# Queries of seven pairs of batches by seven block products for eight (fp32), on one core

## The chip, the cores and the metric

The kernel runs on one core of one Trainium2 chip. The metric is the device time of one execution in microseconds (us), the median of a few runs. The engines are named as in the profile: PE (TensorE, matrix products), DVE (VectorE), ACT (ScalarE), POOL (GpSimd) and SP (SyncE, which issues most transfers). Everything is fp32.

## What is computed

A cross attention for 16 batches of 100 rows of width 640, with 8 heads of 80, against a context of 718 rows of width 384 and 4 more tokens. Cut to what matters:

```
query = hidden_states @ Wq                       # 16 x 100 x 640, Wq 640 x 640
keyt, valt = enc @ Wk, enc @ Wv                  # enc 16 x 718 x 384
hs = mha(query, keyt, valt)
ca_q1 = einsum('btc,th->bch', ca, Wq_ca)[:, indices]
ca_hs1 = mha(ca_q1, residual, residual)          # residual = hidden_states
ca_hs2 = mha(ca_hs1 @ Wq, ca @ Wk_ca, ca @ Wv_ca)
out = (hs + ca_hs2) @ Wout + b_out + residual
```

The change concerns the first line, for batches 2 to 15.

## The kernel before

The program is one list of instructions per engine, in the order in which the code calls them: before the loop a scheduler places them, and from `tc.manual_schedule` (L1235) on each engine keeps the program's order. The loop over the batches b = 0 to 15 is a software pipeline. In stage b PE runs, in this order: the scores of batch b (L609, three groups, queries times keys), then the value products of batch b and the key products of batch b + 1 mixed (L434, L465), the last column chunk of the keys (`last_keys`, L559), in some stages the output projection of two tiles of 128 rows (`project_pair`, L1033 to L1088), in odd stages the queries of the next pair of batches (`queries`, L531 to L551), and the products of the exponentials with the values (a_ps, L1456). The odd stages are b = 1, 3, 5, 7, 9, 11, 13; an output pair is projected in b = 3, 6, 8, 11, 13.

Keys, values and the projection of output pairs already run by schemes with fewer block products: sums of blocks are made ahead (of the context by POOL in `enc_sums`, L481 to L500, thirteen additions per batch; of the weights once), the products go to several PSUM banks, and DVE or ACT add each bank to the results that need it (L403 to L408, `read` in L1059). In `project_pair` DVE makes nine such reads from four banks, and PE goes on in a bank only when its reads are done.

The queries are plain before: `queries` makes one of five chunks of 128 output columns, as five matmuls of 128x128 weights with the rows of both batches (200 columns), and ACT copies the chunk from PSUM to `qp` or, for the fifth, twice with a mask to `qz` (L543, L547). The fifth output chunk holds the last 16 columns of each head.

DVE and POOL in the second half of an odd stage: DVE adds value and key banks, makes the third subtraction of the maximum (`subtract(2)`, L1258, 120 x 1600), then the maximum of the other attention's scores `e1` in steps (`Maximum`, L684 to L730: transpose, reduction, small reductions, spread, transpose) and subtracts it (L815); `softmax1(n)` makes the next n steps. The spread is made by ACT where the other attention's batch follows an output pair, else by DVE (L720 to L727). POOL multiplies and adds values of the small attention (`values2`, L892, L899), issues two loads, makes `keys` (L745, five small products) and then `enc_sums` for the context of batch b + 2. Its next work is `scores1` of the next stage (L798). `enc` is a tile of 15 places of 240 columns: seven for the raw context, which transfers fill, and eight that `enc_sums` fills.

The end of the second half of an odd stage is called in this order (L1390 to L1440): `subtract(2)`, `exponential(2)`, `last_keys`, [`softmax1(3)`, `project_pair`], `softmax1`, `keys`, `enc_sums`, `queries`, `exponentials1`, then a_ps.

Of the kernel before, what the change touches and what calls it, by code (L numbers as in the profile page):

```python
# [10 lines left out]
ALU = mybir.AluOpType  # L11
# [7 lines left out]
P = 128  # L19
# [107 lines left out]
def kernel(  # L127
# [33 lines left out]
    def pair(name):  # L161
        tile = ps2.tile([P, 2, 512], F32, tag="ps2", name=name)
        return tile
# [224 lines left out]
    class Blocks:  # L388


        def __init__(self, plan):
            self.opened, self.begun = {}, set()
            self.plan = iter(enumerate(plan))
            self.ends = {bank: k for k, (bank, _, _) in enumerate(plan)}
# [156 lines left out]
                )  # L551


    def chunk_keys(n, banks, weights, enc):
# [197 lines left out]
    class Second:  # L752
# [56 lines left out]
        def softmax1(self, n=8):  # L809

            if not self.top:
                self.top = Maximum(e1, f"1_{self.b}", self.b - 2 in PAIRS)
            self.top.go(n)
            if self.top.over is not None:
                nc.vector.tensor_tensor(e1[:S], e1[:S], self.top.over[:S], ALU.subtract)  # L815
# [97 lines left out]
    class Last:  # L913
# [109 lines left out]
        def sums(self):  # L1023

            r = PAIRS[self.b]
            one, two = hsTs[r], hsTs[r + 1]
            for out, left, right, op in (
                (sum1, two[:, :2], two[:, 2:4], ALU.add),
                (two[:, :2], sum1, one[:, :2], ALU.subtract),
            ):  # L1030
                nc.gpsimd.tensor_tensor(out, left, right, op)

        def project_pair(self):  # L1033

# [12 lines left out]
            def product(to, terms, first):  # L1047
                steps = [(t[:, c], f[:, c]) for t, f in terms for c in range(t.shape[1])]
                for i, (t, f) in enumerate(steps):
                    nc.tensor.matmul(  # L1050
                        to[:, : H // 2],
                        t,
                        f,
                        start=first and i == 0,
                        stop=i == len(steps) - 1,
                        skip_group_check=True,
                    )

            def read(bank, j, k):  # L1059
                part = xn[r + j][:, k * (H // 2) : (k + 1) * (H // 2)]  # L1060
                nc.vector.tensor_tensor(part, bank[:, : H // 2], part, ALU.add)

            product(b1, [(one[:, :2], w(0, 0))], True)
            read(b1, 0, 0)
            product(b2, [(one[:, 2:4], w(1, 0)), (one[:, 4:], last(0))], True)
            read(b2, 0, 0)
            nc.gpsimd.tensor_tensor(one[:, 2:4], one[:, 2:4], two[:, :2], less)
            product(b1, [(two[:, :2], wout2[:, 0])], False)
            read(b1, 1, 0)
            nc.gpsimd.tensor_tensor(two[:, :2], two[:, 2:4], two[:, :2], less)  # L1070
            nc.gpsimd.tensor_tensor(wout2[:, 0], wout2[:, 0], w(0, 0), less)
# [164 lines left out]
    for b in range(B):  # L1236
# [28 lines left out]
        def exponential(i):  # L1265
            nc.scalar.activation(st[i], st[i], AF.Exp, scale=SCALE)  # L1266
# [60 lines left out]
        elif b + 1 < B:  # L1327
# [61 lines left out]
                m_next = load_m(b + 2)  # L1389
            subtract(2)  # L1390
            exponential(2)
            last_keys(b + 1, enc)
            if b + 2 < B:
                enc_next = load_rest(b + 2, enc_next)
# [1 line left out]
                last.transpose()  # L1396
            if last.b in PAIRS:
                second.softmax1(3)
                last.project_pair()
                if last.b == max(PAIRS):  # L1400
                    nc.sync.dma_start(
                        out=forms[1],
                        in_=wout[: 2 * P, H // 2 :].rearrange("(c p) n -> p c n", p=P),
                    )
            second.softmax1()
        else:
            room = enc_tile("spare").rearrange("p f k -> p (f k)")
            spare.extend(room[:, i * H : (i + 1) * H] for i in range(2))
# [22 lines left out]
            last.project()  # L1431
        if 0 < b < B - 2:
            keys(m_next)
            enc_sums(enc_next)
        if b % 2 and b + 1 < B:
            xT, tiles = xT_at[0], queries_tiles(p + 1)
            for n in range(HC):
                queries(p + 1, xT, tiles, n)
        if 0 < b < B - 1:
            second.exponentials1()  # L1440

# [37 lines left out]
        if b + 2 < B:  # L1479
            second_next.products()  # L1480
            second_next.copy()
        if 0 < b < B - 2:
            mine.turn()
        last = mine
# [55 lines left out]
```

## Time and profile before

| | |
|---|---|
| Median of three runs (lowest, highest) | 925.86 us (924.5 to 927.1) |
| The profiled execution | 925.05 us |
| Its span, first to last instruction | 923.3 us |
| PE busy | 916.2 us, 99% |
| DVE busy | 679.9 us, 74% |
| POOL busy | 682.1 us, 74% |
| ACT busy | 434.2 us, 47% |
| Query products (L535) on PE | 400 records, 69.1 us |

In rows of the profile, `out<-in` are the program's tiles with their numbers left out (enc<-enc is a sum made in the context's tile), then the shapes, the count, and after the bar the busy time, the mean duration of one in ns, and the idle time of the engine before them with what ended it. Rows of the timeline begin with the start and the duration in us, and instructions of one kind that follow each other are merged into one row (x50). PE's fp32 matmuls stand as two records each; PEld is the loading of weights, which runs beside the products. Records of PE overlap, so that the duration of one is longer than its share of PE's time.

### The profile page before, as it was taken

The numbers are of one execution on the slowest core, as the hardware profiler recorded it, in microseconds if no ns is written. First come the engines' busy times: TensorE is split into PE (matmuls) and PEld (weight loads), VectorE is DVE, ScalarE is ACT, GpSimd is POOL, SyncE is SP. The second block draws the span as 40 slices with busy tenths as digits, with TensorE's granted clock in tenths as the row PEclk, the third lists the DMA queues.
The fourth block names the chain that finished last, engine by engine and source line by source line (L and its number), as shares of the span: only waits on it lengthen the run. The fifth ranks groups of instructions, "written<-read, shape, count | busy, mean of one in ns | idle before, by whom it ended". The sixth has DMA issues, their size and how long they took to land.

```text
span 923.3 us, 26190 instructions
## 1 busy us (share of the span) xinstructions
PE 916.2 (99%) x11290; PEld 772.4 (84%) x11290; DVE 679.9 (74%) x1085; ACT 434.2 (47%) x836; POOL 682.1 (74%) x647
## 2 busy tenths in 40 slices
PE   9999999999999999999999999999999999999998
PEld 6988889788797979888798787988879888797866
DVE  2459795888739896795967859579883898838883
ACT  2234543737327373552636536264641737427341
POOL 5749999788947878497784968757996588956723
PEclk9999999999999999999999999999999999999999
DMA  8822013050300404032030310205031050310201
GB/s 258 262 94 78 25 43 100 2 156 2 103 31 13 116 3 131 3 92 65 19 115 4 103 54 30 76 2 154 3 90 43 2 155 2 104 45 2 82 20 41
DMA packets 49675, 62.85 MB, mean 68 GB/s; under 512 B 14072, under 2 KB 38200, under 8 KB 49560
## 3 DMA queue, kind: packets, MB, share of 16 engines
q1 hardware_dynamic: 45512, 51.49, 18.4%
q0 software_dynamic: 3024, 8.53, 3.0%
q8 instruction: 89, 1.46, 0.7%
q10 hardware_dynamic: 1024, 1.15, 0.4%
q14 instruction: 26, 0.21, 0.1%
HBM read 55.59 MB, written 5.57 MB: 66 GB/s over the span
## 4 chain that ended last, share of the span: by engine, by line
PE 96%; DVE 3%; DMA 1%; issue 0%; POOL 0%; ACTq 0%; DVEq 0%; POOLq 0%
PE a_ps L1456 12%; PE s_ps L609 12%; PE v_psA L434 10%; PE v_psB L434 8%; PE kT_ps L559 8%; PE k_psA L465 8%; PE q_ps L535 7%; PE k_psB L465 6%; PE o_ps L1050 5%; PE v_psC L434 3%; PE k_psC L465 3%; PE v_ps L375 2%; PE v_psD L434 2%; PE v_psE L434 2%; PE y_ps L773 1%; PE k_psD L465 1%
## 5 line engine op out<-in xcount | busy, mean ns | idle before, releaser
L798 POOL TENSOR_TENSOR e<-ca,g 100x800 f32<-100x800 f32 x64 | 97.9, 1540 | 125.1 <-ACT kT L407 82.1
L500 POOL TENSOR_TENSOR enc<-enc 128x240 f32<-128x240 f32 x135 | 109.5, 820 | 18.2 <-DMA enc<-in_enct 11.1
L1258 DVE TENSOR_TENSOR st<-st,over 120x1600 f32<-120x1600 f32 x48 | 119.1, 2482 | 0.0
L1456 PEld LDWEIGHTS a_ps<-vs,st 120*36 120x36 f32 (+3 forms) x3072 | 109.2, 125 | 4.9 <-issue 4.8
L1456 PE MATMUL a_ps<-vs,st 120*36 120x81 f32 (+3 forms) x3072 | 112.0, 233 | 0.0
L434 PE MATMUL v_psA<-wv_sb,enc 128*120 128x320 f32 x352 | 109.3, 433 | 0.0
L899 POOL TENSOR_TENSOR hs<-hs,hs 100x640 f32<-100x640 f32 x48 | 100.6, 2095 | 3.8
L805 POOL TENSOR_TENSOR e<-e,e 100x800 f32<-100x800 f32 x48 | 93.6, 1950 | 3.8
L892 POOL TENSOR_TENSOR hs<-vb,p 100x640 f32<-100x640 f32 x64 | 88.0, 1386 | 5.9 <-DMA vb<-va_d 3.0
L434 PE MATMUL v_psB<-wv_sb,enc 128*120 128x320 f32 x296 | 91.9, 433 | 0.0
L1266 ACT ACTIVATE st<-st 120x1600 f32<-120x1600 f32 x48 | 73.9, 1539 | 37.0 <-DVE st L1258 36.9
L465 PE MATMUL k_psA<-enc,wk_sb 128*128 128x240 f32 x360 | 89.2, 371 | 0.0
L434 PEld LDWEIGHTS v_psA<-wv_sb,enc 128*120 128x120 f32 x352 | 64.2, 183 | 25.0 <-issue 0.5
L465 PEld LDWEIGHTS k_psA<-enc,wk_sb 128*128 128x128 f32 x360 | 67.2, 190 | 15.0
L1270 DVE TENSOR_TENSOR most<-most,st 120x800 f32<-120x800 f32 x64 | 67.6, 1056 | 15.9 <-ACT st L659 14.8
L609 PE MATMUL s_ps<-qp,kT 64*56 64x100 f32 (+1 forms) x3072 | 73.5, 248 | 0.0
L465 PE MATMUL k_psB<-enc,wk_sb 128*128 128x240 f32 x300 | 73.0, 366 | 0.0
L434 PEld LDWEIGHTS v_psB<-wv_sb,enc 128*120 128x120 f32 x296 | 54.1, 183 | 21.9 <-DVE vs L405 0.4
L609 PEld LDWEIGHTS s_ps<-qp,kT 64*56 64x56 f32 (+1 forms) x3072 | 67.1, 130 | 5.5 <-issue 4.2
L965 ACT COPY hsT<-turned_hs 32x160 f32<-32x160 f32 (+7 forms) x244 | 67.7, 278 | 3.0
L535 PE MATMUL q_ps<-xT,wq_sb 128*128 128x200 f32 x400 | 69.1, 333 | 0.0
L535 PEld LDWEIGHTS q_ps<-xT,wq_sb 128*128 128x128 f32 x400 | 67.8, 190 | 1.0 <-issue 0.5
(168 smaller groups left out, 1766.1 us busy)
## 6 DMA issues: line engine op xcount, KB each, us to landing
vb<-va_d POOLq DMA_DIRECT2D x32, 250.0 KB, 3.8
vb<-va_d SPq DMA_DIRECT2D x32, 250.0 KB
enc<-in_enct SPq DMA_DIRECT2D x30, 240.0 KB
enc<-in_enct SPq DMA_DIRECT2D x15, 360.0 KB
xT<-in_xt SPq DMA_DIRECT2D x8, 500.0 KB
rest<-in_enct SPq DMA_DIRECT2D x31, 120.0 KB
xn<-in_x SPq DMA_DIRECT2D x11, 320.0 KB
out<-xn SPq DMA_DIRECT2D x11, 320.0 KB
```

What stands on the lines that cost most here:

```text
L434: nc.tensor.matmul(at[0][j][:KN, : H // 2], a_form(self.enc, f)[:, j * KN : (j + 1) * KN], wv_there.get(f, wv_sb[:, W_AT[f]]), start=first ...
L465: nc.tensor.matmul(at[:, i * KT : (i + 1) * KT], wk_sb[:, W_AT[f], i], a_form(self.enc, f), start=(first and i == 0), stop=last, skip_grou ...
L500: nc.gpsimd.tensor_tensor(out, left, right, op)
L535: nc.tensor.matmul(q_ps[:, : 2 * S].rearrange("p (j s) -> p j s", j=2), wq_sb[:, c, n * P : (n + 1) * P], xT[:, :, c, :], start=(c == 0), ...
L609: nc.tensor.matmul(s_ps[at][k0:k1, cols], w, rhs, start=not begun & {(at, k) for k in range(k0, k1, 32)}, stop=last, skip_group_check=True,)
L798: first = nc.gpsimd.tensor_tensor(to, self.ca[:, t, :].unsqueeze(1).to_broadcast([S, NH, S]), g[:, :, t].unsqueeze(2).to_broadcast([S, NH, ...
L805: nc.gpsimd.tensor_tensor(e, e, to, ALU.add)
L892: first = nc.gpsimd.tensor_tensor(to, self.vb[t][:S].rearrange("p (h d) -> p h d", h=NH), p2[:, :, t].unsqueeze(2).to_broadcast([S, NH, D] ...
L899: nc.gpsimd.tensor_tensor(sums, sums, to, ALU.add)
L1258: return nc.vector.tensor_tensor(st[i], st[i], top.over[:KN].unsqueeze(1).to_broadcast([KN, 2, ROWS]), ALU.subtract,)
L1266: nc.scalar.activation(st[i], st[i], AF.Exp, scale=SCALE)
L1456: nc.tensor.matmul(a_v[lo:hi, h % 4], st[i // 2][: KEYS[i], i % 2, h * S + lo : h * S + hi], block(i, h // 4)[: KEYS[i], h % 4], start=(i ...
```

## The change

The queries of batches 2 to 15, two at a time, are made by a scheme of seven products. The four output chunks and the four input chunks of 128 are halved into blocks of 256, and the two batches are the third dimension of two: seven products of a block of weights (`wq_block(g, c)`) with a block of rows take the place of eight. The fifth input chunk (`rest`) is added plainly for each output block and batch, and the fifth output chunk is made plainly for both batches. All matmuls have 64 weight columns, in two halves of the array (k = 0 and 64).

Three sums of weights and four of rows are needed. One of the weights is made once, in place, at the end of b = 0. The other sums are made by DVE for each pair (`sums`: w2, w3, then t1 to t4), in the eight places of the next context's tile that `enc_sums` fills later; so `enc_sums` is now called behind the query products. w2 is renewed once between the products. Without an output pair (b = 1, 5, 7, 9) the six sums stand right behind `subtract(2)` and `exponential(2)`; with one (b = 3, 11, 13) they stand behind the first three reads in `project_pair`: w2 behind the first, w3 behind the second, t1 to t4 behind the third. Of the softmax of the other attention, one step (`between(1)`) stands on DVE behind the renewed w2 and ahead of two additions of results, and the rest behind. Four banks are read by ACT copies, and five additions by DVE bring the other reads. The banks are two pairs and both `psk` banks, where the five chunks before took `psk` and `ps1` banks in turn.

```diff
+    def wq_block(g, c):
+        return wq_sb[:, 2 * c : 2 * c + 2, 2 * g * P : 2 * (g + 1) * P]
+
+    class Queries:
+        def __init__(self, p, xT, enc):
+            self.p, self.xT = p, xT
+            room = enc[:, len(A_RAW) :].rearrange("p f k -> p (f k)")
+            part = lambda lo, n: room[:, lo : lo + 2 * n].rearrange(
+                "p (c n) -> p c n", c=2
+            )
+            self.w2, self.t1 = part(0, 2 * P), part(4 * P, S)
+            lo = 3 * KT
+            self.w3 = part(lo, 2 * P)
+            self.t3, self.t2, self.t4 = (
+                part(lo + 4 * P + 2 * i * S, S) for i in range(3)
+            )
+
+        def v(self, c, m):
+            return self.xT[:, m, 2 * c : 2 * c + 2]
+
+        def sums(self, steps=range(3)):
+            v, less = self.v, ALU.subtract
+            for step in steps:
+                for out, left, right in (
+                    [(self.w2, wq_block(1, 0), wq_block(0, 0))],
+                    [(self.w3, wq_block(1, 1), self.w2)],
+                    [
+                        (self.t1, v(0, 1), v(0, 0)),
+                        (self.t2, v(1, 1), self.t1),
+                        (self.t3, v(1, 1), v(0, 1)),
+                        (self.t4, v(1, 0), self.t2),
+                    ],
+                )[step]:
+                    nc.vector.tensor_tensor(out, left, right, less)
+
+        def product(self, bank, weights, moving, first):
+            steps = [(c, i) for c in range(weights.shape[1]) for i in range(2)]
+            for n, (c, i) in enumerate(steps):
+                for k in (0, 64):
+                    nc.tensor.matmul(
+                        bank[k : k + 64, i * S : (i + 1) * S],
+                        weights[:, c, i * P + k : i * P + k + 64],
+                        moving[:, c],
...
+        def rest(self, bank, g, m, first):
+            weights = wq_sb[:, 4:, 2 * g * P : 2 * (g + 1) * P]
+            self.product(bank, weights, self.xT[:, m, 4:], first)
+
+        def make(self, tiles, between):
...
+            one = pair(f"q_ps1_{p}")
+            two = pair(f"q_ps2_{p}")
+            a, b = psumk(f"q_psA_{p}"), psumk(f"q_psB_{p}")
+            f, c, e, d = one[:, 0], one[:, 1], two[:, 0], two[:, 1]
...
+            def add(bank, g, m):
+                nc.vector.tensor_tensor(q(g, m), full(bank), q(g, m), ALU.add)
+
+            for ch in range(HC):
+                for k in (0, 64):
+                    nc.tensor.matmul(
+                        full(f)[k : k + 64],
+                        wq_sb[:, ch, 4 * P + k : 4 * P + k + 64],
+                        self.xT[:, :, ch, :],
...
+            for u in range(2):
+                nc.scalar.mul(
+                    qz[:, 0, :, u * S : (u + 1) * S], full(f), qmask[:, u : u + 1]
+                )
+            self.product(a, w(0, 0), v(0, 0), True)
+            nc.scalar.copy(q(0, 0), full(a))
+            self.rest(c, 0, 0, True)
+            self.product(c, w(0, 1), v(1, 0), False)
+            add(c, 0, 0)
+            self.product(a, self.w2, self.t2, False)
+            nc.vector.tensor_tensor(self.w2, w(0, 1), self.w2, ALU.subtract)
+            between(1)
+            self.rest(e, 1, 0, True)
+            self.product(e, w(1, 1), self.t4, False)
+            nc.scalar.copy(q(1, 0), full(e))
+            add(a, 1, 0)
+            self.product(b, self.w3, self.t3, True)
+            add(b, 1, 0)
+            self.rest(d, 0, 1, True)
+            self.product(d, self.w2, v(1, 1), False)
+            nc.scalar.copy(q(0, 1), full(d))
+            self.rest(b, 1, 1, False)
+            nc.scalar.copy(q(1, 1), full(b))
+            between(8)
+            self.product(a, w(1, 0), self.t1, False)
+            add(a, 0, 1)
+            add(a, 1, 1)
...
@@ class Second, softmax1
+            if self.top.over is not None:
+                return
             self.top.go(n)
...
@@ class Last, project_pair
-        def project_pair(self):
+        def project_pair(self, others):
+            others = iter(others)
...
                 nc.vector.tensor_tensor(part, bank[:, : H // 2], part, ALU.add)
+                for other in others:
+                    other()
+                    break
...
@@ the loop
             subtract(2)
             exponential(2)
+            if b % 2:
+                mixed = Queries(p + 1, xT_at[0], enc_next[0])
+                if last.b not in PAIRS:
+                    mixed.sums()
             last_keys(b + 1, enc)
...
-                last.project_pair()
+                last.project_pair(
+                    [lambda n=n: mixed.sums([n]) for n in range(3)] if b % 2 else []
+                )
...
-            second.softmax1()
+            if b % 2:
+                second.softmax1(1 if last.b in PAIRS else 3)
+            else:
+                second.softmax1()
...
         if 0 < b < B - 2:
             keys(m_next)
-            enc_sums(enc_next)
         if b % 2 and b + 1 < B:
             xT, tiles = xT_at[0], queries_tiles(p + 1)
-            for n in range(HC):
-                queries(p + 1, xT, tiles, n)
+            mixed.make(tiles, second.softmax1)
+        if 0 < b < B - 2:
+            enc_sums(enc_next)
...
+        if b == 0:
+            nc.vector.tensor_tensor(
+                wq_block(1, 0), wq_block(1, 0), wq_block(1, 1), ALU.add
+            )
```

More of the change, by code (lines that the diff above doesn't have):

```diff
@@ L551, in queries, with q, full @@
                 )
+    def wq_block(g, c):
[37 more added lines that the diff above has]
+                        moving[:, c],
+                        start=first and n == 0,
+                        stop=n == len(steps) - 1,
+                        skip_group_check=True,
+                    )
[3 more added lines that the diff above has]
+        def make(self, tiles, between):
+            qp, qz = tiles
+            p, v, w = self.p, self.v, wq_block
+            one = pair(f"q_ps1_{p}")
+            two = pair(f"q_ps2_{p}")
+            a, b = psumk(f"q_psA_{p}"), psumk(f"q_psB_{p}")
+            f, c, e, d = one[:, 0], one[:, 1], two[:, 0], two[:, 1]
+            def q(g, m):
+                return qp[:, g, :, m * S : (m + 1) * S]
+            def full(bank):
+                return bank[:, : 2 * S].rearrange("p (i s) -> p i s", i=2)
+            def add(bank, g, m):
[6 more added lines that the diff above has]
+                        self.xT[:, :, ch, :],
+                        start=(ch == 0),
+                        stop=(ch == HC - 1),
+                        skip_group_check=True,
+                    )
[26 more added lines that the diff above has]
+            add(a, 1, 1)
@@ L1398 @@
                 second.softmax1(3)
-                last.project_pair()
+                last.project_pair(
+                    [lambda n=n: mixed.sums([n]) for n in range(3)] if b % 2 else []
+                )
                 if last.b == max(PAIRS):
@@ L1481 @@
             second_next.copy()
+        if b == 0:
+            nc.vector.tensor_tensor(
+                wq_block(1, 0), wq_block(1, 0), wq_block(1, 1), ALU.add
+            )
         if 0 < b < B - 2:
```

## The prediction

> **What bounds the kernel now.** I read the page first (span, busy shares, granted clock, chain), then the chain in order of time, then the timeline of single stages. The profiled execution took 925.05 us, of which the span is 923.3; it lies 0.8 us under the median of 925.86. All sums are made against 925.05. About 0.3%, 2.8 us, is what a measurement of this kernel can tell from no change.
>
> ```profile
> span 923.3 us, 26190 instructions
> PE 916.2 (99%) x11290; PEld 772.4 (84%) x11290; DVE 679.9 (74%) x1085; ACT 434.2 (47%) x836; POOL 682.1 (74%) x647
> PEclk9999999999999999999999999999999999999999
> PE 96%; DVE 3%; DMA 1%; issue 0%; POOL 0%; ACTq 0%; DVEq 0%; POOLq 0%
> ```
>
> TensorE is busy for 99% of the span at full granted clock, and the chain that ended last is 96% PE. So two things alone move the end: less PE work, and a wait put in front of PE. DVE and POOL each have a quarter free, but only where nothing is due.
>
> **PE work.** The query projection and its neighbours:
>
> ```profile
> 357.60 8.46 PE q_ps L535 x50
> 366.06 6.92 PE a_ps L1456 x191
> L609 PE MATMUL s_ps<-qp,kT 64*64 64x100 f32 x1536 | 73.4, 248 | 0.0
> ```
>
> Each fp32 matmul stands as two records. A pair of batches takes 25 full matmuls of 200 columns: 50 records in 8.46 us, 0.338 per matmul. The change needs, in halves of 64 weight columns that run beside each other: 5 of 200 columns for the fifth output chunk, 8 of 100 for the fifth input chunk (`rest`), and 7 products of 4 each for the rest, 36 of 100 in all. No row shows 128x64 weights with 100 columns. The nearest: a_ps runs such halves with 81 columns, 96 record pairs in 6.92 us, 0.072 each; q_ps has 0.169 per record at 200. A line through both gives 0.0875 at 100 columns, 0.175 per matmul. By the column rate of q_ps it would be 0.169; by s_ps, whose 3072 records run four at a time, 73.4/768 = 0.096, so 0.191. I take 0.175, as a_ps has the same tiles. That makes 5 x 0.338 + 36 x 0.175 = 7.99 us against 8.46: **-0.47 us per pair, -3.3 for seven** (ends: -4.8 and +0.8). A product of four is 0.70, a `rest` 0.35. From the start Q of the query stage the order is: fifth output chunk until Q+1.69, product a 2.39, rest and product c 3.44, second product on a (needs w2, t2) 4.14, rest and product e (t4) 5.19, product b (w3, t3) 5.89, rest d 6.24, product d (needs the renewed w2) 6.94, rest b (needs DVE's read of b) 7.29, last product 7.99.
>
> **Who must keep up.** DVE now makes six sums ahead (two of 512 elements, four of 200), renews w2 and adds five results. This is b = 5, an odd stage without an output pair:
>
> ```profile
> 352.68 2.86 DVE L1258 TENSOR_TENSOR st<-st,over 120x1600 f32<-120x1600 f32 x1
> 353.94 3.02 POOL L899 TENSOR_TENSOR hs<-hs,hs 100x640 f32<-100x640 f32 x1
> 355.46 1.00 DVE L700 STREAM_TRANSPOSE turned<-e 128x800 f32<-128x800 f32 x1
> 357.44 8.62 PE L535 MATMUL q_ps<-xT,wq_sb 128*128 128x200 f32 x50
> 358.58 1.40 POOL L745 TENSOR_TENSOR m<-mb,hmask 128x64 f32<-128x64 f32 x5 [0.59 <-DMA mb<-m_d]
> 359.33 0.33 ACT L543 COPY qp<-q_ps 128x200 f32<-128x200 f32 x1 [0.87 <-PE q_ps L535]
> 359.60 0.99 DVE L727 COPY spread<-mx 128x800 f32<-128x800 f32 x1
> 365.99 6.99 PE L1456 MATMUL a_ps<-vs,st 120*64 120x81 f32 x192
> 384.56 1.54 POOL L798 TENSOR_TENSOR e<-ca,g 100x800 f32<-100x800 f32 x1 [13.44 <-ACT kT L407]
> ```
>
> The steps of the softmax that come ahead of the spread take 359.60 - 355.46 = 4.14 us, and all now stand behind the six sums. A reader starts 0.20 us after PE leaves a product (357.44 + 1.69 against 359.33). What decides is how DVE and POOL share:
>
> ```profile
> 671.08 3.04 POOL L932 TENSOR_TENSOR xn<-xn,bias 128x640 f32<-128x640 f32 x2
> 671.48 4.32 DVE L1258 TENSOR_TENSOR st<-st,over 120x1600 f32<-120x1600 f32 x1
> 676.52 1.81 DVE L1258 TENSOR_TENSOR st<-st,over 120x1600 f32<-120x1600 f32 x1
> 32.03 5.28 POOL L745 TENSOR_TENSOR m<-m,hmask 128x64 f32<-128x64 f32 x1 [0.56 <-PE y_ps L773]
> 34.72 2.43 DVE L522 TENSOR_TENSOR wk_sb<-wk_sb 128x256 f32<-128x256 f32 x7
> ```
>
> The same subtraction takes 1.81 us alone and 4.32 where it meets two POOL operations: they end at 674.12, and it ends 1.7 us later. The other way round, one of POOL's keys, of which five take 1.40 us above, stands for 5.28 while DVE runs a row of copies and sums. So a DVE operation with both operands in SBUF and a POOL operation exclude each other whole, and the engine that goes on back to back keeps its turn. The new sums are of this kind; the transposes, and reads of PSUM, are not. The Trainium skill, SBUF — State Buffer, section "SBUF: two separate sides", says the same: the pair of ports is "an exclusive lock, not a bandwidth split". By that rule, which these rows bear out, the sums speak against the change.
>
> Sizes: 320 elements take 0.49 (the reads L1061 below), 1600 take 1.81, hence 1.03 ns each: 0.69 for 512 and 0.37 for 200.
>
> **b = 5, 7, 9.** POOL's L899 has waited since 353.94 and takes the port when the subtraction ends, until 356.96. Before, DVE went on with transposes beside it; now the first sum waits. w2 357.65, w3 358.34, t1 358.71. POOL's keys (1.40, due 358.58) come next: t2 to t4 end at 361.22 behind them, 359.82 ahead of them. Softmax +4.14, first addition and renewed w2 +1.06: 366.42 or 365.02. Product d is due at Q+6.24 = 363.68; it ends 367.12 or 365.72. Spread (0.99) and two additions (0.74) then hold `rest` b until 368.15 or 366.75, and 1.05 more brings a_ps to 369.20 or 367.80 instead of 365.99: +3.2 or +1.8, the saving already inside. I take +2.6 each, **+7.8**; the keys stand back to back as L932 did, which is the late case.
>
> **b = 3, 11, 13.** Here the sums stand between DVE's reads of the output pair (L1061); b = 3:
>
> ```profile
> 245.42 0.49 DVE L1061 TENSOR_TENSOR xn<-o_ps,xn 128x320 f32<-128x320 f32 x1 [0.56 <-issue]
> 245.66 1.54 POOL L899 TENSOR_TENSOR hs<-hs,hs 100x640 f32<-100x640 f32 x1
> 248.13 0.49 DVE L1061 TENSOR_TENSOR xn<-o_ps,xn 128x320 f32<-128x320 f32 x1 [0.66 <-PE o_ps L1050]
> 248.25 0.74 POOL L1067 TENSOR_TENSOR hsT<-hsT,hsT 128x256 f32<-128x256 f32 x1
> 248.93 1.24 PE L1050 MATMUL o_ps<-wout_sb,sum 128*128 128x320 f32 x4
> 249.06 0.72 POOL L1070 TENSOR_TENSOR hsT<-hsT 128x256 f32<-128x256 f32 x1
> 249.74 1.54 POOL L1071 TENSOR_TENSOR wout<-wout,wout_sb 128x640 f32<-128x640 f32 x1
> 250.01 2.85 PE L1050 MATMUL o_ps<-wout_sb,hsT 128*128 128x320 f32 x10
> 250.21 1.57 DVE L1061 TENSOR_TENSOR xn<-o_ps,xn 128x320 f32<-128x320 f32 x3 [1.59 <-PE o_ps L1050]
> 251.24 1.41 POOL L745 TENSOR_TENSOR m<-mb,hmask 128x64 f32<-128x64 f32 x5
> 253.78 8.62 PE L535 MATMUL q_ps<-xT,wq_sb 128*128 128x200 f32 x50
> 262.33 1.90 PE L1456 MATMUL a_ps<-vs,st 120*64 120x81 f32 x48
> ```
>
> L899 holds the port until 247.20, so w2 ends 247.89 and the second read 248.38. w3 ends 249.68 behind L1067, 249.07 ahead of it; the third read 250.17 or 249.56. PE's product with `sum1` (248.93) must wait for that read, as it goes on in the same bank. Then t1 to t4 (1.48) meet L1070, L1071 and the keys (0.72 + 1.54 + 1.41 = 3.67), which stand back to back. Behind all of them the sums end at 254.83 and the fourth read at 255.32; right behind L1070, at 252.50. The last product in that bank, two matmuls into the 2.85 us row and so at 251.09 before, starts at the fourth read's end: +4.2 or +1.4. In the query stage DVE is late again: renewed w2 Q+5.03, transpose and subtraction of the softmax 7.02 (7.70 if a sum of POOL's goes first), two additions 7.76 (8.44), and 1.05 more is 8.81 (9.49) against 262.33 - 253.78 = 8.55: +0.3 or +0.9. I take 3.5 + 0.6 = 4.1 each, near the late end for POOL's row of operations, and the same for 11 and 13: **+12.3** (ends 1.7 and 5.1 each).
>
> **b = 1.** POOL's value products come later against PE here:
>
> ```profile
> 135.84 1.81 DVE L1258 TENSOR_TENSOR st<-st,over 120x1600 f32<-120x1600 f32 x1
> 136.02 3.04 POOL L899 TENSOR_TENSOR hs<-hs,hs 100x640 f32<-100x640 f32 x1
> 139.14 1.27 POOL L892 TENSOR_TENSOR hs<-vb,p 100x640 f32<-100x640 f32 x1
> 140.49 8.65 PE L535 MATMUL q_ps<-xT,wq_sb 128*128 128x200 f32 x50
> 149.06 6.98 PE L1456 MATMUL a_ps<-vs,st 120*64 120x81 f32 x192
> ```
>
> w2 starts at 139.06 and ends 139.75; an L892 (1.27) until 141.02; w3 and t1 until 142.08; an L899 (1.54) until 143.62; t2 to t4 until 144.73, or 147.54 if two more of POOL's go between. By the same steps (+4.14, +1.06, then 2.78 to the end) a_ps starts at 152.71 or 155.52 instead of 149.06: +3.7 or +6.5. I take **+4.4**, near the early end, since sums that don't wait for each other keep the port.
>
> **Edits costed at nothing.** POOL's sums for the next context, now behind the query products, start some 5 us later plus the waits; POOL idles 13.44 us before 384.56, which covers it, and without that cover the next keys' products would wait. ACT reads six times per pair, as before (four copies, two masked). The one sum at the end of b = 0 is 0.69 us of DVE while PE runs scores. The softmax of the second attention ends some us later, but its result is first read by z_ps, behind a_ps (6.92 us) and the scores. No DMA is moved in its queue.
>
> **Sum:** 7.8 + 12.3 + 4.4 = 24.5, so 925.05 + 24.5 = **949.5 us**. The ends: 5.4 + 5.1 + 3.7 = 14.2 gives 939, 9.6 + 15.3 + 6.5 = 31.4 gives 956.5.
>
> **Rivals.**
> - *The sums find the port free* (POOL's operations slide behind them). Then they take 2.86 us; b = 5 ends at 366.38 (+0.4, the spread still stands ahead of the additions), b = 1 gains its 0.47, b = 3 loses 0.3: 3 x 0.4 - 0.47 + 3 x 0.3 = +1.6, **926.6**. The rows of 671.48 and 32.03 speak against it.
> - *Faster: seven products for eight come through.* Were DVE never late, PE would keep 0.47 seven times: **921.8**. It decides wherever the six sums and the softmax steps are done by Q+6.24; in b = 5 they miss by 1.3 us at the least.
> - *The clock falls.* If PE, after waiting 3.5 us in four stages, ran as long at half clock, each would cost 1.75 more: +7, **956.5**. No wait of that length is in this trace, and the granted clock is full throughout. The Trainium skill, TensorE: Matmul & The Clock Gate, section "Why this matters for your kernels", asks for "No PE-idle gaps >~3µs between matmul bursts"; no run here shows it.
>
> **How the numbers follow.** My forecast has 0.76, the free port 0.10, the gain 0.06, the clock 0.08. The range 935 to 958 holds the forecast's ends and the clock, about 0.8; the free port and the gain are left out. Faster by over 0.3%: 0.06; within: 0.10, the free port; slower: 0.84.
>
> **What would show it.** In the changed kernel (its own line numbers): sums of L590 of over 1 us beside POOL's value products; PE waiting in o_ps for the reads L1175 in b = 3, 11, 13, and before product d and the last `rest` in every odd stage; even stages unchanged; the PE records of a query stage adding to some 8.0 us without the waits. Wrong would be: sums of 0.69 and 0.37 throughout, or waits of PE in even stages.

## The result

The changed kernel takes 946.52 us (median of 6 runs, 943.21 to 948.39), the kernel before 924.54 us on the same chip: ratio 1.0234, 95% interval 1.021 to 1.0258. It is slower by 22 us. 949.5 us was forecast, with a range of 935 to 958.

The page of the changed kernel's profiled execution (945.73 us) has these lines; the last one is the chain that ended last, by engine:

```profile
span 944.0 us, 27936 instructions
...
PE 918.3 (97%) x12088; PEld 767.2 (81%) x12088; DVE 743.5 (79%) x1170; ACT 434.3 (46%) x836; POOL 688.5 (73%) x647
...
PEclk9999998999999999999999999999999999999999
...
PE 73%; POOL 11%; DVE 11%; issue 2%; DMA 1%; ACT 1%; ACTq 0%; DVEq 0%; POOLq 0%
```

PE held 96% of the chain before; now POOL and DVE hold 11% each. PE's busy time hardly moved (916.2 to 918.3 us), and it contains a stretch at a lower clock (the 8 in the row of the granted clock), so the sum of busy time does not show what the products save. The view of one line shows what the products of the queries (L596) waited for, in us and times:

```profile
  DVE enc L646: 5.7, 4
  DVE qp L624: 5.4, 6
  ACT qz L637: 1.1, 7
  DVE enc L590: 0.8, 1
```

L646 renews w2, L624 adds a result bank, L590 are the six sums, L637 are ACT's masked copies. A gap between records shows less than is lost: in b = 5 below, the three gaps are 1.59 us, the work is 7.92 us (the same stage in the last run below, where nothing waits), and the stage takes 10.18 us from its first product to a_ps, so each gap stands for some 0.22 us more. What counts is therefore the time from one stage's first a_ps to the next stage's. In change against the kernel before, in us:

| stages | forecast | measured |
|---|---|---|
| 1 | +4.4 | +6.7 |
| 5, 7, 9 | +2.6 each | +2.2, +1.3, +1.7 |
| 3, 11, 13 | +4.1 each | +3.4, +3.2, +3.5 |
| even stages, 2 to 14 | 0 | +0.7 to -0.4 |
| up to the first a_ps of b = 0 | 0 | -1.7 |

The last row isn't the change: ahead of that point nothing is changed, and in the runs below it is anywhere from -2.2 to +2.6. Without it the change costs 22.4 us. Of b = 5's +2.2, 0.46 us are a gap ahead of z_ps in which PE waited for nothing that the profile shows ("issue"); the query stages of b = 5, 7 and 9 take 10.18 us each, against 8.55 before.

**b = 5.** The timeline of PE, then that of DVE, then that of POOL (start and duration in us; the idle time before a row and its releaser stand in brackets):

```profile
366.73 1.91 PE L628 MATMUL q_ps<-xT,wq_sb 128*64 128x200 f32 x20
...
369.49 1.25 PE L596 MATMUL q_ps<-xT,wq_sb 128*64 128x100 f32 x24 [0.16 <-ACT qz L637]
...
374.19 0.91 PE L596 MATMUL q_ps<-xT,enc 128*64 128x100 f32 x16 [0.70 <-DVE enc L646]
375.83 0.56 PE L596 MATMUL q_psB<-xT,wq_sb 128*64 128x100 f32 x8 [0.73 <-DVE qp L624]
...
376.91 1.29 PE L1582 MATMUL a_ps<-vs,st 120*64 120x81 f32 x32
```

```profile
361.88 2.86 DVE L1375 TENSOR_TENSOR st<-st,over 120x1600 f32<-120x1600 f32 x1
364.66 2.04 DVE L590 TENSOR_TENSOR enc<-wq_sb 128x512 f32<-128x512 f32 x1
...
368.91 1.00 DVE L811 STREAM_TRANSPOSE turned<-e 128x800 f32<-128x800 f32 x1
...
373.04 0.37 DVE L624 TENSOR_TENSOR qp<-q_ps,qp 128x200 f32<-128x200 f32 x1
373.32 0.81 DVE L646 TENSOR_TENSOR enc<-wq_sb,enc 128x512 f32<-128x512 f32 x1
...
375.41 0.37 DVE L624 TENSOR_TENSOR qp<-q_psB,qp 128x200 f32<-128x200 f32 x1
```

```profile
363.13 3.01 POOL L1012 TENSOR_TENSOR hs<-hs,hs 100x640 f32<-100x640 f32 x1
...
367.67 1.77 POOL L856 TENSOR_TENSOR m<-mb,hmask 128x64 f32<-128x64 f32 x5 [0.49 <-DMA mb<-m_d]
```

The subtraction ends at 364.74 and the first sum at 366.70: it stands as 2.04 us and needs 0.69, because POOL's value product (until 366.14) has the port. The five further sums then follow each other until 368.9. Only then come the softmax (L811 to 373.0), the first addition and the renewed w2, which ends at 374.13: PE starts product d at 374.19. POOL's five keys were not a block in front of the last sums but stood between them (1.77 us instead of 1.40).

**b = 3.** PE in the output pair (L1164) and before the last `rest`, then the sums of DVE:

```profile
255.66 1.34 PE L1164 MATMUL o_ps<-wout_sb,sum 128*128 128x320 f32 x4 [0.73 <-DVE xn L1175]
...
258.97 1.85 PE L1164 MATMUL o_ps<-wout_sb,hsT 128*128 128x320 f32 x6 [0.89 <-POOL m L856]
...
261.83 1.91 PE L628 MATMUL q_ps<-xT,wq_sb 128*64 128x200 f32 x20
...
270.34 0.56 PE L596 MATMUL q_psB<-xT,wq_sb 128*64 128x100 f32 x8 [1.06 <-DVE qp L624]
...
271.42 0.80 PE L1582 MATMUL a_ps<-vs,st 120*64 120x81 f32 x18
```

```profile
251.66 1.92 DVE L590 TENSOR_TENSOR enc<-wq_sb 128x512 f32<-128x512 f32 x1
...
253.91 1.29 DVE L590 TENSOR_TENSOR enc<-wq_sb,enc 128x512 f32<-128x512 f32 x1
...
256.04 1.58 DVE L590 TENSOR_TENSOR enc<-xT,enc 128x200 f32<-128x200 f32 x1
...
258.35 1.27 DVE L1175 TENSOR_TENSOR xn<-o_ps,xn 128x320 f32<-128x320 f32 x3
```

Three of the six sums wait for POOL, and the reads that PE needs stand behind them. The second wait is put down to POOL's key product, but PE uses nothing of that: it goes on in the bank as soon as the first of the three reads (258.35) is done.

**b = 1.** The six sums and POOL's value products take turns here, and then the clock falls. The timelines of DVE, of POOL and of PE, and two windows of time (start and end, length, the busy time of PE, PEld, DVE, ACT and POOL with the number of instructions, then the granted clock, the DMA share and GB/s):

```profile
135.90 2.04 DVE L590 TENSOR_TENSOR enc<-wq_sb 128x512 f32<-128x512 f32 x1
137.97 1.64 DVE L590 TENSOR_TENSOR enc<-wq_sb,enc 128x512 f32<-128x512 f32 x1
139.54 1.70 DVE L590 TENSOR_TENSOR enc<-xT 128x200 f32<-128x200 f32 x1
...
144.18 0.54 DVE L590 TENSOR_TENSOR enc<-xT,enc 128x200 f32<-128x200 f32 x1
```

```profile
134.19 3.19 POOL L1012 TENSOR_TENSOR hs<-hs,hs 100x640 f32<-100x640 f32 x1
137.46 1.60 POOL L1005 TENSOR_TENSOR hs<-vb,p 100x640 f32<-100x640 f32 x1
139.14 1.87 POOL L1012 TENSOR_TENSOR hs<-hs,hs 100x640 f32<-100x640 f32 x1
```

```profile
138.87 1.91 PE L628 MATMUL q_ps<-xT,wq_sb 128*64 128x200 f32 x20
...
150.34 1.60 PE L596 MATMUL q_ps<-xT,enc 128*64 128x100 f32 x16 [3.63 <-DVE enc L646]
...
154.03 2.16 PE L1582 MATMUL a_ps<-vs,st 120*64 120x81 f32 x34
```

```profile
145.45:148.87 3.42, 1.26 (x30) 1.06 (x26) 3.21 (x11) 0.33 (x1) 3.32 (x9) 1.00 0.78 234
148.87:155.69 6.82, 5.32 (x66) 5.01 (x68) 5.49 (x9) 1.52 (x3) 4.63 (x7) 0.50 0.01 2
```

Each sum gets through when a POOL operation has ended: w2 ends at 137.94 behind 137.38, w3 at 139.61 behind 139.06, t1 at 141.24 behind 141.01, and so on until 144.72. Product d, for which PE waited 3.63 us, then takes 1.60 us instead of 0.91: the granted clock is 0.50 from 148.87, while PE still waits, to 155.69, behind the first a_ps. Not all of that is lost. From product d to a_ps b = 1 takes 3.69 us and b = 5, at full clock, 2.72, so 1.0 us of the stage's +6.7 is the clock; the 1.66 us at half clock behind the first a_ps cost another 0.8, which is b = 2's +0.7. Of the other five runs four have a mean granted clock of 0.998 and one 1.000, where this one has 0.996.

### The profile page after: what moved, and what is told of

It reads as the page before. It is cut to its first block, busy times and chain, and to the rows that moved or that the text cites. A ratio compares the mean times of both kernels' runs of the same rounds, so it can differ in the third digit from the quotient of the medians.

```text
span 944.0 us, 27936 instructions
## 1 busy us (share of the span) xinstructions
PE 918.3 (97%) x12088; PEld 767.2 (81%) x12088; DVE 743.5 (79%) x1170; ACT 434.3 (46%) x836; POOL 688.5 (73%) x647
## 4 chain that ended last, share of the span: by engine, by line
PE 73%; POOL 11%; DVE 11%; issue 2%; DMA 1%; ACT 1%; ACTq 0%; DVEq 0%; POOLq 0%
PE a_ps L1582 12%; PE s_ps L720 11%; PE v_psA L434 7%; PE v_psB L434 6%; PE k_psA L465 6%; PE kT_ps L670 5%; PE k_psB L465 4%; PE o_ps L1164 3%; PE v_psC L434 3%; POOL e L909 2%; DVE enc L590 2%; POOL e L916 2%; DVE st L1375 2%; PE v_ps L375 2%; POOL hs L1005 2%
## 5 line engine op out<-in xcount | busy, mean ns | idle before, releaser
L776 ACT COPY st<-s_ps 120x800 f32<-120x800 f32 x64 | 49.8, 829 | 35.4 <-PE s_ps L720 35.4
L465 PEld LDWEIGHTS k_psB<-enc,wk_sb 128*128 128x128 f32 x300 | 57.0, 190 | 7.7
```

What stands on the lines that cost most here:

```text
L465: nc.tensor.matmul(at[:, i * KT : (i + 1) * KT], wk_sb[:, W_AT[f], i], a_form(self.enc, f), start=(first and i == 0), stop=last, skip_grou ...
```

## The experiments

The theory is that of the prediction: the sums exclude POOL's operations, so they end late, and everything queued behind them on DVE (softmax, additions, renewed w2, reads of the output pair) comes late for PE, while the seven products themselves save PE half a microsecond a pair. The rivals: DVE is overloaded whatever POOL does; the new form on PE (halves, banks, additions) costs by itself; the clock. Each ratio is to the kernel before on the same chip.

### The sums without the port

```diff
-                    nc.vector.tensor_tensor(out, left, right, less)
+                if step == 0:
+                    turn(self.room[:, :512], wq_sb[:, 2, :512])
+                elif step == 1:
+                    turn(self.room[:, 736:1248], self.room[:, :512])
+                else:
+                    turn(self.room[:, 512:736], flat[:, :224])
...
```

(`turn` is DVE's transpose; three more of 224 follow.)

> The six sums ahead of the queries are replaced by six DVE transposes of the same places and nearly the same sizes (512 and 224 elements), which run beside POOL; the products read what the transposes leave, so queries are wrong and only the time is read. DVE has the same number of instructions in the same order, about 0.4 us less work a stage. Theory (the sums exclude POOL's operations and wait behind them): the row of sums shrinks to some 2.5 us in every odd stage, the wait of 3.6 us in b = 1 and the waits in o_ps and before product d go, and some 0.3 us a stage is left: about 927 us (924 to 931). Rival (DVE simply has too many instructions ahead of product d, whatever POOL does): the waits shrink by the 0.4 us at most, 943 to 946 us.

928.87 us, ratio 1.0052 (1.0034 to 1.0069). DVE in b = 1 of this kernel:

```profile
137.25 0.70 DVE L583 STREAM_TRANSPOSE enc<-wq_sb 128x512 f32<-128x512 f32 x1
137.99 0.71 DVE L585 STREAM_TRANSPOSE enc<-enc 128x512 f32<-128x512 f32 x1
138.62 0.37 DVE L587 STREAM_TRANSPOSE enc<-xT 128x224 f32<-128x224 f32 x1
```

Six instructions of the sizes of the sums, in the same place of DVE's order, take 0.70 and 0.37 us while POOL multiplies (its products there take 1.28 to 1.55). DVE's load in front of product d is nearly what it was without the waits, and the loss is 5.5 us in the medians instead of 22.0: b = 1 costs +0.7 instead of +6.7, b = 5, 7 and 9 within 0.4 of before, b = 3, 11 and 13 +1.3 to +2.0, of which 1.06 us is the wait before the last `rest`, behind the softmax. What the transposes do not do is read two operands from SBUF. So it is the port, and the rival of an overloaded DVE falls.

### No sums at all

```diff
-                    nc.vector.tensor_tensor(out, left, right, less)
...
-            nc.vector.tensor_tensor(self.w2, w(0, 1), self.w2, ALU.subtract)
...
```

> The six sums and the renewal of w2 are left out, and the products read the stored weights and inputs instead, so queries are wrong and only the time is read. PE's instructions, PSUM banks, copies and additions are those of the changed kernel. Theory (all of the loss comes from the sums' place on DVE): the gain of PE's 0.5 us a pair shows, less some 0.4 us a stage in which the first rest waits for ACT's masked copies: 922 to 925 us. Rival (the products in halves, the banks or the five additions cost by themselves): it stays above 930 us.

924.52 us, ratio 1.0000 (0.9986 to 1.0014; the median before on this chip is 923.36). The form on PE does not cost anything by itself that these runs show. But it does not bring 3 us either: PE waits in each of the seven stages for ACT's masked copies (0.16 us in the records, 0.33 from start to start: in b = 5 of the changed kernel 1.02 us lie between 368.47, the start of product a, and 369.49, of which the product takes 0.69). And b = 3, 11 and 13 are still 0.9 to 1.6 us longer than before: there PE stands 1.26, 1.24 and 0.56 us ahead of s_ps and z_ps, long before the query stage, for nothing that the profile shows. The kernel of the next section, with plain queries, has such a gap of 1.39 us in its a_ps. Where these gaps come from is open.

### Only the halves

```diff
-                wq_sb[:, c, n * P : (n + 1) * P],
+                    wq_sb[:, c, n * P + k : n * P + k + 64],
```

(in the kernel before, for k = 0 and 64 in turn)

> The kernel before with one edit: each plain query matmul of 128 weight columns is issued as two halves of 64 columns, nothing else. Theory (two halves of 64 columns run beside each other and cost what one of 128 does): 924.5 us, within 1 us. Rival (a half has a price of its own, 0.01 us more per pair of halves as in my line through a_ps and q_ps at 100 columns): +0.3 us a pair of batches, 927 us.

924.57 us, ratio 1.0006 (0.9993 to 1.0019). The 800 records have a median of 332 ns, the 400 of the kernel before 333 ns: twice the records in the same time (b = 5's query stage takes 8.51 us, 8.55 before), so two halves run beside each other and cost what a whole one does.

### Other banks

```diff
-            f, c, e, d = one[:, 0], one[:, 1], two[:, 0], two[:, 1]
+            f, e, c, d = one[:, 0], one[:, 1], two[:, 0], two[:, 1]
```

> The changed kernel with f and c in two different pair tiles, so that the first rest on bank c no longer waits for ACT's masked copies of f (about 0.38 us a stage of seven). Theory (DVE is what PE waits for later in the same stage, so this wait only hides part of that one): the later waits grow by as much as this one shrinks, 946.5 us, within 1 us. Rival (the waits add up): 7 x 0.38 = 2.7 us less, 943.8 us.

944.93 us, ratio 1.0216 (1.0194 to 1.0238): not to be told from the changed kernel, but by the time alone not from the rival's 943.8 us either. The profile decides. The gaps behind ACT are gone, and the later ones in the same stages are longer (three gaps of 1.86 us in b = 5, where the changed kernel has 1.59, the one behind ACT among them); from the start to the last a_ps the loss is 20.2 us, against 20.7. A wait of PE ahead of another one that DVE ends is free.

### The queries of b = 1 plain

```diff
-            mixed.make(tiles, second.softmax1)
+            if b == 1:
+                for n in range(HC):
+                    queries(p + 1, xT, tiles, n)
+            else:
+                mixed.make(tiles, second.softmax1)
...
```

> The changed kernel, but the pair of b = 1 is made by the plain products of the kernel before (the sum of two weight blocks is made at the end of b = 1 for that). Theory (the 6.7 us of b = 1 are the wait for the renewed w2 behind sums and softmax, with the fall of the clock behind that wait): that stage is as before, the other six as in the changed kernel, 946.5 - 6.7 = 939.8 us, and no stretch at a lower granted clock. Rival (b = 1 only takes up time that a later stage would otherwise lose): 943 us or more.

941.7 us, ratio 1.0185 (1.0166 to 1.0204). Stage 1 is as before (0.0), the six others cost what they cost in the changed kernel (+3.3, +1.8, +1.4, +1.7, +3.5, +3.3), and the clock is full in the whole profile. From the first to the last a_ps the change costs 15.1 us instead of 22.4. The median is 1.9 us over the expectation, and why is not shown; the profiled execution (942.78 us, the slowest of the four) has 2.6 us ahead of the first a_ps, where nothing is changed.

### The sums behind the output pair

```diff
-                last.project_pair(
-                    [lambda n=n: mixed.sums([n]) for n in range(3)] if b % 2 else []
-                )
+                last.project_pair([])
+                if b % 2:
+                    mixed.sums()
```

> The changed kernel, but in b = 3, 11 and 13 the six sums stand behind the reads of the output pair instead of between them. Theory (PE's waits of 1.6 us in o_ps are these sums): the waits in o_ps go, and as the sums are still done ahead of the first product that needs them, 1.6 to 2.5 us a stage are won, the wait of 1.06 us before the last rest remains: 946.5 - 6 = 940.5 us (939 to 942). Rival (the sums just move the wait into the query stage): 945 to 947 us.

941.04 us, ratio 1.0181 (1.0166 to 1.0197), as expected. In b = 3, the first two sums:

```profile
262.84 0.68 DVE L590 TENSOR_TENSOR enc<-wq_sb 128x512 f32<-128x512 f32 x1
263.56 0.69 DVE L590 TENSOR_TENSOR enc<-wq_sb,enc 128x512 f32<-128x512 f32 x1
```

The same instructions that took 1.92 and 1.29 us take 0.68 and 0.69 where POOL has nothing to do. PE loads its weights from `wq_sb` at that moment, so that is not what made them long. PE no longer waits in o_ps, and the three stages cost +1.3, +1.3 and +1.2: the wait before the last `rest` (1.07 us), which stands behind the softmax, is left.

### The softmax behind the additions

```diff
-            between(1)
             self.rest(e, 1, 0, True)
...
-            between(8)
             self.product(a, w(1, 0), self.t1, False)
             add(a, 0, 1)
             add(a, 1, 1)
+            between(8)
```

(and no step of it ahead of the query products in odd stages, but for those ahead of `project_pair`)

> The changed kernel, but in the odd stages the softmax steps of the second attention stand behind the last additions of the queries instead of ahead of and between them. Theory (PE waits for w2 and for bank b because the softmax is ahead of them on DVE): the waits before product d and the last rest go in b = 5, 7 and 9 (1.3 us each) and the one of 1.06 us in b = 3, 11 and 13; b = 1 keeps only what its sums lose to POOL, some 2.5 of its 6.7 us: 946.5 - 3.9 - 3.2 - 4.2 = 935 us (933 to 938). Rival (the softmax becomes late for z_ps, which then waits as long): 943 us or more.

943.09 us, ratio 1.02 (1.0182 to 1.0218): 8 us over what the theory expected, and in the rival's range, but by luck, as z_ps does not wait for DVE. The waits before product d and the last `rest` are gone in all stages, as expected, b = 5, 7 and 9 now cost +0.1, -0.6 and -0.2, and b = 1 costs +1.0 (2.5 was expected). But a wait that I had named on neither side took their place. What the line of y_ps (L883) waited for in this kernel, and one place:

```profile
  DVE hs_sb L1595: 7.7, 4
```

```profile
379.81 1.50 PE L883 MATMUL y_ps<-m,xT 128*64 128x72 f32 x20 [1.90 <-DVE hs_sb L1595]
```

y_ps needs the bank of the first half of a_ps, DVE reads that bank (L1595), and this read now stands behind the softmax. And the clock: two windows at that wait, then two at the wait of 1.90 us that ends at 496.15, with PE's busy time behind the length and the granted clock third from the end:

```profile
376.61:380.02 3.41, 1.51 (x44) 1.37 (x40) 3.20 (x6) 0.87 (x1) 1.44 (x3) 1.00 0.00 0
380.02:383.44 3.42, 3.42 (x72) 3.25 (x71) 2.20 (x6) 0.37 (x1) 0.00 (x0) 0.50 0.02 5
...
492.66:496.07 3.41, 1.60 (x46) 1.42 (x41) 3.24 (x5) 0.59 (x1) 1.73 (x3) 1.00 0.00 0
496.07:499.49 3.42, 3.34 (x104) 3.15 (x108) 2.45 (x6) 0.65 (x2) 0.00 (x0) 1.00 0.02 5
```

Behind the first wait PE has half the clock for some 3.4 us, so 1.7 us are lost; behind the other the clock stays full. It fell after three of the four waits of 1.9 to 2.0 us. The stages b = 2, 6, 8 and 10, in which this is counted, cost +3.7, +3.6, +2.0 and +3.7: the one without the fall is 1.6 us cheaper.

### The four edits together

b = 1 plain, the sums behind the output pair, the softmax behind the additions, the other banks.

> The four edits together: b = 1 plain, the sums of b = 3, 11 and 13 behind the reads of the output pair, the softmax steps of the odd stages behind the additions, f and c in different pair tiles. Theory (the new form saves PE 0.5 us a pair wherever DVE is on time, and with this order it is): no wait of PE over 0.3 us in a query stage, 6 x 0.5 = 3 us less than before, 920.5 us on a chip where the kernel before takes 923.5 (ratio 0.9968, 0.995 to 0.999). Rival (something of the loss stays: softmax late for z_ps, or POOL's sums for the next context late for its products): ratio 1.000 to 1.005.

932.05 us, ratio 1.0085 (1.0069 to 1.0101). The theory's number missed again, by the same wait, and the ratio is over the rival's range too. From the softmax to y_ps in b = 5 of the profiled execution, which took 927.5 us:

```profile
370.24 0.99 DVE L927 TENSOR_TENSOR e<-e,over 100x800 f32<-100x800 f32 x1
...
371.36 0.49 DVE L1597 TENSOR_TENSOR hs_sb<-a_ps,rs 100x320 f32<-100x320 f32 x1
...
371.99 0.94 PE L883 MATMUL y_ps<-m,xT 128*64 128x72 f32 x20 [1.91 <-DVE hs_sb L1597]
```

Three such waits are 5.7 us. No wait is left in the query stages, and the six with the new form are the faster for it (-0.1 to -0.7 each in this run). Of the six runs the one with a mean granted clock of 1.000 is the shortest (a span of 925.8 us); the others have 0.998 (928.5 us), 0.996 (930.3 and 931.9) and 0.994 (930.4 and 930.9). One fall of 3.4 us at half clock in a span of 926 us lowers the mean by 0.0018, so these would be none, one, two and three falls, of 1.7 us each. That is most of the differences, though not their order; and that the falls came at the three waits is not shown, as there is a trace of the first run alone.

### The softmax between the additions

```diff
+            between(1)
             add(c, 0, 0)
...
-            between(1)
...
-            between(8)
+            between(2)
             self.product(a, w(1, 0), self.t1, False)
```

(for b = 5, 7 and 9; the rest as in the four edits)

> As the four edits together, but in b = 5, 7 and 9 the softmax steps stand between the additions (the first transpose ahead of the first addition, the next two steps behind the second one, the rest behind the last), not all behind the last. Theory (the 1.9 us before y_ps in these three stages are the read of a_ps behind the softmax on DVE; and the runs of 930 to 934 us beside one of 927.5 are the clock at half for some 3.4 us after such a wait): the waits before y_ps go, 3 x 1.9 = 5.7 us less than the profiled run of the four edits, and with no wait over 1 us the clock stays full in every run: 921.8 us (920.5 to 923), ratio to the kernel before 0.9975 (0.996 to 0.999). Rival for the clock (it falls in this kernel whatever PE waits for): runs spread by 3 us and more again, with mean clocks under 0.998. Rival for the time (the softmax between the additions makes these late): waits before the last rest and 924 us or more.

923.17 us in 12 runs, the kernel before 925.11 in 17: ratio 0.9979 (0.9966 to 0.9993). Its page:

```profile
span 921.8 us, 27705 instructions
...
PE 97%; DMA 1%; issue 0%; POOL 0%; DVE 0%; ACTq 0%; SPq 0%; POOLq 0%
```

and the ends of its query stage in b = 5:

```profile
355.91 1.91 PE L628 MATMUL q_ps<-xT,wq_sb 128*64 128x200 f32 x20
...
363.83 2.36 PE L1587 MATMUL a_ps<-vs,st 120*64 120x81 f32 x62
```

That is 7.92 us from start to start without a wait, against 8.55 before. In the chain's rows, by which the prediction counted, it is 355.98 to 364.00, 8.02 us against 8.46. The waits before y_ps in these stages are gone, and no run's mean clock is under 0.999. The runs still spread by 4.2 us (921.56 to 925.78), and those of the kernel before by 6.6, so the clock is not all that spreads them.

This version is 0.2% faster than the kernel before: six pairs by 0.44 us would be 2.6 us; 1.9 are left in the medians. The one profile does not show that gain as a whole. b = 5, 7 and 9 are 0.5 to 1.0 us shorter than before, but b = 3, 11 and 13 are 0.2 to 0.5 us longer and b = 12, 14 and 15 0.4 to 0.6, so that the time from the first a_ps to the last is 0.3 us longer; the 1.8 us by which this execution gains lie ahead of the first a_ps, where nothing is changed. In b = 3, 12, 13, 14 and 15 PE stands 0.28 to 0.91 us ahead of s_ps or z_ps for nothing that the profile shows, and in b = 11 1.08 us ahead of y_ps, put down to POOL's sums for a context. Why is open.

## Why the prediction was right

**The port, right.** Sums of 1.3 to 2.0 us beside POOL and of 0.68 away from it, transposes of the same size undisturbed, and 22.0 us of loss that shrink to 5.5 without the port: the forecast's mechanism. With it fall the two rivals in which DVE is in time (926.6 and 921.8 us). They come near only in kernels of another order: 923.17 us in the last run.

**PE's work, right.** 7.99 us were forecast for a pair, 8.02 measured in the same chain's rows (8.46 before). I chose the line through a_ps; a record of L596 has a median of 249 ns with overlap, and the halves alone cost nothing.

**b = 5, 7, 9: too large.** +2.6 was taken, between +1.8 and +3.2; +1.3 to +2.2 was measured by stages, two of the three under the low end, and +1.6 in each of the three query stages alone. The step that failed is that the keys stand back to back in front of t2 to t4. They ran between the sums. The early case was nearer; the chain of steps behind it (softmax 4.14, addition and w2 1.06, the rest 1.05) held.

**b = 3, 11, 13: somewhat too large.** +4.1 taken, +3.2 to +3.5 measured, inside 1.7 to 5.1. For the output pair 3.5 was taken, 2.1 to 2.3 measured (in b = 3 11.91 us from its first product to the first of the queries, 9.69 before). The sums lost the port three times, not to all of POOL's row. The query stage cost 1.0 instead of 0.6 (9.59 us from 261.83 to 271.42, 8.55 before).

**b = 1: too small, and a rival came true in it.** +4.4 was taken, near the early end of +3.7 to +6.5, "since sums that don't wait for each other keep the port". They did not keep it. From the start of the query stage (138.87) the last sum ends after 5.85 us, where the early case has 4.24 (144.73 - 140.49) and the late one 7.05: this step failed. By the forecast's own steps behind it, 5.85 us make +5.3. On top of it the clock fell in the wait of 3.63 us and cost 1.0 us of this stage and 0.8 of the next. Of the stage's +6.7 some 5.7 are then the sums. Of the clock rival the mechanism is right; it was given four stages and came in one, and it needs neither 3.5 us nor the 3 us that the prediction quotes, since 1.9 was enough three times out of four.

**Missed:** the wait for ACT's masked copies, 0.33 us in seven stages. f and c are halves of one pair tile, and PE's first matmul into c waits for the reads of f. The prediction counted ACT's reads but not the tile that they hold. It was free in the changed kernel, since DVE ended the later waits, and costs when these are gone.

**An edit costed at nothing that was not free.** "Its result is first read by z_ps" was the whole check on a later softmax. It holds for the result, but the instructions that stand behind the softmax on DVE, the reads of a_ps, come late too, and y_ps waits for them. In the changed kernel the softmax was late by less than the length of a_ps and nothing showed; with it moved further back, it cost 1.9 us a stage.

The terms that were too large (by 2.6 and 2.3 us in the two groups) and the one too small (by 2.3) partly cancel, and the even stages add 0.5: 24.5 us forecast, 22.4 measured without the start. And 1.8 of the 22.4 are the fall of the clock, which no term of the sum holds. So the mechanism was right, but that 949.5 us lies only 3 us from the measured 946.52 is in part luck.

## What to carry to other kernels

Before work is given to an engine with a quarter of its time free, look at what the engine that shares its port does at that moment, and at each instruction queued behind: here 2.86 us of sums a stage cost 22 us in seven stages, and in another place and order six of them cost next to nothing (-1.0 to +0.5 us a stage). Moving a step later is checked not by its own reader alone but by every instruction that it then stands in front of. Where PE is the bound, a saving of half a microsecond a stage is worth having only if no wait is added, and short waits of PE are dearer than they look, as the clock can fall behind them.

## What the runs showed of the hardware

- **Half the clock after waits under 2 us.** Stretches of some 3.4 us at 0.50 followed three of four PE waits of 1.9 to 2.0 us in one profile and none of three in another. With the other banks none followed waits of 1.82 and 2.59 us in b = 1, but a stretch (374.08 to 377.50 us) began in the third of three gaps of 0.77, 0.36 and 0.73 us, while the changed kernel's pairs of 0.70 and 0.73 us had none. So a wait's length alone does not decide it.
- **The granted clock changes on a grid.** With the softmax behind the additions it changes at 158.16, 161.57, 380.02, 383.44, 612.13 and 615.54 us, which are 1, 64, 1, 67 and 1 steps of 3.413 us. In the other profiles, too, its changes lie whole numbers of such steps apart. The Trainium skill, TensorE: Matmul & The Clock Gate, section "Part 1: The HAM clock gate (the "warmup" mystery)", speaks of a free-running activity window of about 3.4 us, and the steps agree. In the window of the grid right ahead of a fall PE stood idle, by its records, for 0.56, 0.56 and 0.58 of the time (softmax behind the additions), 0.63 (changed kernel) and 0.73 (sums behind the output pair); windows with 0.53 to 0.54 (the fourth wait there, and two in the four edits) were followed by none. The kernel with the other banks does not fit: 0.57 without a fall and 0.48 with one. That a wait counts by its share of such a window is thus likely, but no run was made to test it.
- **Who gets the port next is not settled.** In b = 1 DVE's sums and POOL's products took turns one by one; in b = 5 POOL had nothing to multiply between 366.14 and 367.67, and from then on its short keys stood between the sums. Turns would fit both, but not the prediction's rows at 671.48 and 32.03. The prediction's rule, that an engine which goes on back to back keeps its turn, is refuted by b = 1; no run was made that puts another in its place.
- **A gap in PE's records is shorter than the loss**, by 0.2 us each here, so that losses are better read from the starts of a later tile than added up from gaps.
